# A Trainium2 kernel for channel attention, linear attention and a routed layer: some transposed tiles moved inside SBUF by 16 transfers on two queues, and image 0's loads cut smaller

## The chip, the core and the metric

The kernel runs on one core of one Trainium2 chip. The metric is the device time of one launch in microseconds, the median of several runs. The profile is of one more execution, whose own time stands beside its span.

Short names are those of the profile: PE is the matrix engine (TensorE) and PEld its weight loads, DVE the vector engine, ACT the scalar engine, POOL the GpSimd engine, SP the engine that issues most DMAs. ACT can issue DMAs too. SBUF is the on-chip memory of 128 partitions, PSUM the matmul's accumulator.

## The reference

The input x is four images of 32 channels with 128 by 128 pixels. Layer 0 folds each 2 by 2 patch into channels, normalises an energy matrix, takes a softmax and adds the weighted sum:

```python
xs = x.reshape(B, C, h, R, w, R).transpose(0, 1, 3, 5, 2, 4).reshape(B, C * R * R, h, w)
...
q = xs.reshape(B, C * R * R, hw)
energy = jnp.einsum('bci,bcj->bij', q, q)
d = jnp.sqrt(jnp.diagonal(energy, axis1=1, axis2=2))
energy = energy / (d[:, :, None] * d[:, None, :])
attn = jax.nn.softmax(energy, axis=-1)
out = jnp.einsum('bcj,bij->bci', q, attn).reshape(B, C * R * R, h, w)
out = gamma * out + xs
```

So the energy of an image is 4096 by 4096 and symmetric. Layer 1 takes the result as 4096 tokens of 128 numbers an image, and has a normalised linear attention without softmax, then a second normalisation and a layer of eight experts of which each token takes the two best:

```python
t = t + _L1_attn_ref(_ln_t(t), L1_attn_Wk, L1_attn_Wq, L1_attn_Wv)
t = t + _L1_ffn_ref(_ln_t(t), L1_ffn_router_w, L1_ffn_router_b, L1_ffn_expert_w, L1_ffn_expert_b)
```

## The kernel before

**Layer 0, `attend` (L417).** The 4096 positions of an image are cut into eight columns of 512. For row i (0 to 7) the loop takes the pairs (i, jc) with jc from 0 to i. A pair has four steps j. A step makes one product of 128 by 512 (`pe`, L556), its exponential on ACT (`pr`, L559, with the row sums), and two steps later a matmul of `pr` with the values into `po` (L440). Since the energy is symmetric, the other half of the matrix is the transpose of what is there: for jc < i each `pr` is also transposed in blocks of 32 by 32 by DVE into a tile `F` (L566, the profile shows L369 of a helper), and when the pair is complete the blocks must change places across partitions, which makes the tile `G`. `transposed_share` (L371) then takes four more steps: a matmul with `G` (`pg`, L375) and an ACT instruction that sums `G` (`junk`, L380); the last one adds `pg` to the sum of column jc (L385). The blocks on the diagonal (jc = i) go a smaller way of the same kind (`move_diagonal`, `bring_diagonal`).

**How F becomes G.** `move` (L470) comes two steps after the last `pr` of the pair. It writes `F` to DRAM in one transfer of 1 MiB (`blocks`, L483). Three steps later `bring` (L488) reads it back in four transfers of 256 KiB (L491), each for one quarter of the partitions, in the order that `G` needs. All five are issued by SP. The last image's row 7 has another way for jc of 3 or more (L471 to L481): 16 transfers of 64 KiB from `F` to `G` inside SBUF, all by SP.

**What sets the order.** The order of PE, DVE, ACT and SP is written out by hand: each engine runs its instructions in the order in which the Python loop emits them. `tick` counts steps; `after(n, f)` puts f into the n-th step from now. `clock` counts work in units of a quarter of a matmul: a step of a full pair adds 8, and a step of a transposed share 4 more. A share waits in the list `late` until its due clock, `LAG` = 57 units after `bring`; at most one step of a share goes beside each step of a pair, and the list is first in, first out. `F`, `G` and the DRAM tile `blocks` are rings of 3, 3 and 4 buffers.

**Other work beside it.** The generators in `timed` (L1318 to L1330) are spread over an image: each is given a begin and an end in per cent of the image's clock and a count of turns. Among them are `prep` (loads and norms of the next image, DMAs at L279), `input_rows` (L593; loads the residual T, four parts of 8 rows of tokens, each in four transfers of 128 KiB), and, in image 0 alone, `setup_weights` (46 to 58%) and `setup_sorting` (L136), which fills two DRAM tiles `xs` with rows of x in eight transfers of 624 KiB, DRAM to DRAM, issued by ACT (L154). From 84% on, layer 1 of the image begins (`layer1`) and runs on beside layer 0 of the next one, a turn each 10 units of clock: norms, attention, router, then a sort by expert with indirect DMAs by POOL (L988, L1113), loads of sorted tiles by SP (L1012), products (L1048), stores (L1034), loads of partial sums by ACT (L1089) and the stores of the output (L1095).

The lines that the change touches: L152 to L155 (`xs`), L482 to L486 (`move`), L595 to L596 (`input_rows`), L1325 and L1330 (`timed`).

Of the kernel before, what the change touches and what calls it, by code (L numbers as in the profile page):

```python
# [12 lines left out]
F32 = mybir.dt.float32  # L13
# [9 lines left out]
def kernel(  # L23
# [43 lines left out]
    nc = tc.nc  # L67
    P = 128
    B, C, H, W = x.shape
# [4 lines left out]
    NJ = CH // P  # L74
    HW2 = W // 2
    KT = 32
    S = 32
# [11 lines left out]
    gpool = ctx.enter_context(tc.tile_pool(name="gpool", bufs=3))  # L89
# [29 lines left out]
    NT = 2 * HR + E - 1  # L119
# [6 lines left out]
    xs = [dram.tile([NT * P, D], F32, tag=f"xs{h}", name=f"xs_{h}", bufs=1) for h in range(2)]  # L126
    xs_made, xs_read = ([], []), ([], [])
# [8 lines left out]
    def setup_sorting():  # L136
        def iota(dst, pattern, part=0):
            nc.gpsimd.iota(
                dst, pattern=pattern, base=0, channel_multiplier=part, allow_small_or_imprecise_dtypes=True
            )  # L140

        iota(rank_below, [[1, P]], part=-1)
        nc.vector.tensor_scalar(rank_below, rank_below, 0.0, None, ALU.is_gt)
        iota(upto, [[1, E], [-1, E]])
        nc.vector.tensor_scalar(upto, upto, 0.0, None, ALU.is_ge)
        iota(tiles_of[:, 0, :], [[P, HR]])
        iota(tile_no[:, :, 0], [[1, NT]])
        yield
        yield

        rows = x.rearrange("b c h w -> (b c h) w")
        step = NT * P // 4  # L152
        for g in range(8):
            inst = nc.scalar.dma_start(xs[g // 4][ts(g % 4, step), :], rows[ts(g, step), :])  # L154
            xs_made[g // 4].append(inst.ins)  # L155
            yield
            yield

# [19 lines left out]
    def idle(n):  # L178
        for _ in range(2 * n):
            yield  # L180
# [90 lines left out]
    def tokens(ap, b):  # L271
        return ap[b].rearrange("c (s k r) w -> s r c k w", s=2, r=2)

    def load_tokens(dst, b, k0, nk, queues=(nc.sync, nc.sync)):
        src = tokens(x, b)
        for s in range(2):
            for r1 in range(2):
                p0 = s * 64 + r1 * 32
                queues[r1].dma_start(dst[p0 : p0 + 32], src[s, r1, :, k0 : k0 + nk, :])  # L279
# [72 lines left out]
    clock = [0]  # L352
    tick = [0]
    queued = []
    late = []
    LAG = 57
# [4 lines left out]
    def after(ticks, f):  # L361
        queued.append((tick[0] + ticks, f))
# [8 lines left out]
    def transposed_share(b, st, i, jc, G):  # L371

        pg = ps_g.tile([P, CH], F32, tag="pg", name=f"pg_{b}_{i}_{jc}")
        for ib in range(NJ):
            nc.tensor.matmul(  # L375
                pg.rearrange("p (a f) -> p a f", a=4), st["qT"][i][:, ib, :], G[:, :, ib],
                start=(ib == 0), stop=(ib == NJ - 1),
            )
            junk = work.tile([P, 4, P], BF16, tag="junk", name=f"junk_{b}_{i}_{jc}_{ib}", bufs=1)
            nc.scalar.activation(  # L380
                junk, G[:, :, ib], AF.Copy, accum_out=st["sums"][:, NJ * i + ib, jc : jc + 1]
            )
            if ib == NJ - 1:
                o = st["o"][jc].rearrange("p (j a c) -> p a j c", a=4, c=S)
                nc.vector.tensor_tensor(o, o, pg.rearrange("p (a j c) -> p a j c", a=4, c=S), ALU.add)  # L385
                st["got"][jc] += 1
            yield "done" if ib == NJ - 1 else None
# [29 lines left out]
    def attend(b, st):  # L417
# [11 lines left out]
        for i in range(NCH):  # L429
# [40 lines left out]
            def move(F, i, jc):  # L470
                last = b == B - 1 and i == NCH - 1 and jc >= NCH - 5  # L471
                if last:
                    G = gpool.tile([P, 4, NJ, P], F32, tag="G", name=f"G_{b}_{i}_{jc}")
                    for a in range(4):
                        for q in range(4):
                            nc.sync.dma_start(
                                G[ts(q, S), a].rearrange("p ib f -> p (ib f)"),
                                F[ts(a, S), q].rearrange("p ib j c -> p (ib j c)"),
                            )
                    late.append((clock[0] + 58, transposed_share(b, st, i, jc, G)))  # L480
                    return  # L481
                blocks = dram.tile([4, S, 4, CH], F32, tag="blocks", name=f"blocks_{b}_{i}_{jc}", bufs=4)  # L482
                nc.sync.dma_start(  # L483
                    blocks.rearrange("a p q f -> (a p) q f"), F.rearrange("p q ib j c -> p q (ib j c)")
                )
                after(3, partial(bring, blocks, i, jc))  # L486

            def bring(blocks, i, jc):  # L488
                G = gpool.tile([P, 4, NJ, P], F32, tag="G", name=f"G_{b}_{i}_{jc}")
                for q in range(4):  # L490
                    nc.sync.dma_start(  # L491
                        G[ts(q, S)].rearrange("p a ib f -> p a (ib f)"), blocks[:, :, q].rearrange("a p f -> p a f")
                    )
                late.append((clock[0] + LAG, transposed_share(b, st, i, jc, G)))
# [33 lines left out]
            for jc in order:  # L528
# [15 lines left out]
                if jc < i and not both:  # L544
                    F = fpool.tile([P, 4, NJ, NJ, S], F32, tag="F", name=f"F_{b}_{i}_{jc}")
                    Fb = F.rearrange("p q ib j c -> p ib q j c")
                elif jc == i and not ending:
                    F = fpool.tile([P, 4, 6, S], F32, tag="F", name=f"F_{b}_{i}_{i}")
# [33 lines left out]
    def finish():  # L582

        while queued or late:
            yield
            tick[0] += 1
            turn_tick()
            clock[0] += 3 * NJ
            step_share()
            yield  # L590


    def input_rows(b, st):  # L593
        st["T"] = T = big1.tile([P, KT, D], F32, tag="T", name=f"T_{b}")
        for kc in range(4):  # L595
            load_tokens(T[:, ts(kc, 8), :], b, 8 * kc, 8)  # L596
            yield
            yield
            yield from idle(1)
# [703 lines left out]
    states = [{} for _ in range(B)]  # L1303
# [14 lines left out]
    timed = [(first, 0, 1, 4)]  # L1318
    for b in range(B):

        if b == 0:
            for kc, begin, end in ((1, 0, 5), (2, 6, 20), (3, 25, 45)):
                timed.append((prep(0, kc, states[0]), begin, end, 12))
            timed.append((setup_weights(), 46, 58, 9))
            timed.append((setup_sorting(), 58, 98, 9))  # L1325
        if b + 1 < B:
            nxt = states[b + 1]
            timed.append((prep(b + 1, 0, nxt), 65, 82, 13))
            timed.append((prep(b + 1, 1, nxt), 83, 99, 13))
        timed.append((input_rows(b, states[b]), *((55, 75) if b in (0, B - 1) else (82, 99)), 9))  # L1330
        done = [0] * len(timed)
        start = clock[0]
        closing = None
        for half, _ in enumerate(chain(attend(b, states[b]), finish() if b == B - 1 else ())):
            if half % 2 == 0:
                t = 100 * (clock[0] - start) / UNITS
                moved = []
                if closing is None and t > 84:
                    closing = layer1(b, states[b])
                    steady.append([closing.first_parts() if b == B - 1 else closing.all_parts(), clock[0]])  # L1340
                for n, (steps, begin, end, count) in enumerate(timed):
                    if t >= begin and done[n] * (end - begin) < (t - begin) * count:
                        moved.append(steps)
                        done[n] += 1
                for stream in steady:
                    if clock[0] >= stream[1]:
                        stream[1] = clock[0] + PACE
                        moved.append(stream[0])
            for steps in moved:
                next(steps, None)  # L1350
        for steps, *_ in timed:
            for _ in steps:
                pass
        timed = []
        if b + 1 < B:
            timed.append((prep(b + 1, 2, nxt), 2, 20, 13))
            timed.append((prep(b + 1, 3, nxt), 30, 50, 13))
# [43 lines left out]
```

## Time and profile before

| What | Value |
|---|---|
| Median of 3 runs | 1744.91 us (1744.48 to 1747.42) |
| The profiled execution's own time | 1753.19 us |
| Its span, first to last instruction | 1751.4 us |
| Mean granted TensorE clock | 0.983 |
| Ends of row 7 (`o`, L445) in images 0 to 3 | 378.2, 791.6, 1209.0, 1638.8 us |
| DMA moved | 355.24 MB; HBM read 183.64 MB, written 173.15 MB |
| DMAs by SP's queue (q1) | 314.91 MB, 64.0% of 16 engines' span |
| DMAs by POOL's queue (q0) | 25.19 MB, 5.1% |
| DMAs by ACT's queue (q10) | 13.77 MB, 2.7% |

The page cuts the span in 40 slices and gives a digit for each: the busy share in tenths, and 9 is 90% or more. The list of waits has for each line the engine and its waiting instruction, then what ended the wait, and after the colon the total in us, how often, and the longest. A line of the timeline has the start, the duration in us, engine, line, operation, the tiles (output before the arrow), how many instructions it merges, and in brackets the idle time before and what ended it. SPq and ACTq are DMA issues; their durations are those of the issue, not of the transfer. A wait for several semaphores is put down to the one that came last.

The rows of image 0 end at 21.7, 34.2, 59.6, 97.5, 145.7, 213.5, 294.5 and 378.2 us, those of image 1 from row 4 on at 537.4, 602.4, 690.2 and 791.6, of image 2 at 953.0, 1016.8, 1105.2 and 1209.0, of image 3 at 1369.8, 1434.0, 1527.8 and 1638.8. So the three rows named in the change, 5 to 7, take some 230 to 270 us of each image.

### The profile page before, as it was taken

How to read it: one execution, taken by the hardware profiler on the slowest of the kernel's cores; microseconds unless marked ns; L12 is line 12 of the kernel's file. 1: busy time of each engine (PE TensorE's matmuls, PEld its weight loads, DVE VectorE, ACT ScalarE, POOL GpSimd, SP SyncE). 2: the span in 40 equal slices, each digit the busy share in tenths (PEclk: the TensorE clock that was granted, in tenths of full speed). 3: DMA queues.
4: the chain of work that ended last, by engine and by line, in shares of the span. 5: the costliest groups of instructions: out<-in, count | busy, mean ns of one | idle time of the engine just before them, and what ended most of it. 6: DMA issues, size and time to landing. Idle time of an engine off the chain costs nothing. (4 is left out here: it accounts for less than half of the span.)

```text
span 1751.4 us, 21197 instructions
## 1 busy us (share of the span) xinstructions
PE 1667.8 (95%) x5458; PEld 882.2 (50%) x5458; DVE 939.7 (54%) x2443; ACT 927.0 (53%) x2893; POOL 512.0 (29%) x553
## 2 busy tenths in 40 slices
PE   8999998999999999899999999979999999899887
PEld 5444444455554455445554455535555455444633
DVE  4433333467485335566477334546748533455687
ACT  3555444466565555446565455536556455445376
POOL 1000000011026505540015622552102660463166
PEclk9999999999999999999999999989999999999989
DMA  4675877776568799997567799998656889995001
GB/s 136 195 207 166 217 200 222 237 212 190 165 195 239 232 276 252 264 243 197 164 189 223 227 273 264 251 244 224 192 166 196 251 223 271 265 267 133 1 13 37
DMA packets 240168, 355.24 MB, mean 203 GB/s; under 512 B 26928, under 2 KB 154928, under 8 KB 226096
## 3 DMA queue, kind: packets, MB, share of 16 engines
q1 hardware_dynamic: 219792, 314.91, 64.0%
q0 software_dynamic: 12288, 25.19, 5.1%
q10 hardware_dynamic: 7968, 13.77, 2.7%
q8 instruction: 46, 0.75, 0.2%
q14 instruction: 74, 0.61, 0.1%
HBM read 183.64 MB, written 173.15 MB: 204 GB/s over the span
## 5 line engine op out<-in xcount | busy, mean ns | idle before, releaser
L559 ACT ACTIVATE pr<-pe 128x512 f32<-128x512 f32 (+1 forms) x576 | 322.3, 560 | 546.3 <-PE pe L556 427.9
L440 PE MATMUL po<-pr,qT 128*128 128x512 f32 (+3 forms) x1152 | 553.2, 562 | 3.9 <-ACT o L445 3.5
L375 PE MATMUL pg<-G,qT 128*128 128x512 f32 x880 | 456.8, 601 | 37.5 <-DMA G<-blocks 25.6
L556 PE MATMUL pe<-qn,qn 128*128 128x512 f32 x896 | 464.7, 601 | 1.9 <-ACT pr L559 1.6
L369 DVE STREAM_TRANSPOSE F<-pr 128x512 f32<-128x512 f32 x440 | 305.9, 702 | 169.6 <-ACT pr L559 152.2
L440 PEld LDWEIGHTS po<-pr,qT 128*128 128x128 f32 x1152 | 217.1, 192 | 252.6 <-issue 224.8
L380 ACT ACTIVATE junk<-G 128x512 bf16<-128x512 f32 x440 | 273.1, 621 | 33.9 <-DMA G<-blocks 27.3
L375 PEld LDWEIGHTS pg<-G,qT 128*128 128x128 f32 x880 | 167.3, 192 | 239.6 <-issue 205.8
L1113 POOL DMA_INDIRECT yb<-ys,place x192 | 185.1, 964 | 275.6 <-DMA xn<-xs 103.2
L988 POOL DMA_INDIRECT xs<-xn,place x192 | 185.6, 967 | 125.5 <-issue 51.6
L556 PEld LDWEIGHTS pe<-qn,qn 128*128 128x128 f32 x896 | 156.0, 193 | 113.9 <-issue 103.5
L385 DVE TENSOR_TENSOR o<-o,pg 128x512 f32<-128x512 f32 x110 | 75.4, 685 | 201.4 <-PE pg L375 170.1
L164 POOL TENSOR_TENSOR rn<-ss,neg_half 128x8 f32<-128x8 f32 (+1 forms) x17 | 27.8, 1634 | 401.6 <-DVE ss L325 401.6
L559 ACT ACTIVATION_READ_ACCUMULATOR pr<-pe 128x1 f32 x576 | 112.1, 195 | 0.0
L1022 ACT ACTIVATE xn<-pys 128x256 f32<-128x256 f32 (+1 forms) x120 | 44.9, 376 | 116.1 <-PE pys L1055 69.3
L1048 PEld LDWEIGHTS pys<-ew_sb,xn 128*128 128x128 f32 x468 | 67.9, 191 | 57.2 <-issue 45.3
L164 POOL TENSOR_TENSOR rsf<-dm_f,neg_half 128x8 f32<-128x8 f32 (+1 forms) x15 | 26.2, 1746 | 235.1 <-DVE sv_f L635 235.1
L556 PE MATMUL pe<-qn 128*128 128x512 f32 (+3 forms) x256 | 90.2, 435 | 0.7 <-ACT qn L344 0.7
L380 ACT ACTIVATION_READ_ACCUMULATOR junk<-G 128x1 f32 x440 | 84.4, 192 | 0.0
L1048 PE MATMUL pys<-ew_sb,xn 128*128 x468 | 71.8, 276 | 11.4 <-ACT xn L1022 5.4
L1031 DVE COPY result<-pys 128x256 f32<-128x256 f32 (+1 forms) x60 | 24.6, 410 | 101.6 <-ACT xn L1022 46.2
L164 POOL TENSOR_TENSOR rsa<-dm_a,neg_half 128x8 f32<-128x8 f32 x16 | 26.4, 1647 | 167.4 <-DVE sv_a L635 167.1
(189 smaller groups left out, 1618.5 us busy)
## 6 DMA issues: line engine op xcount, KB each, us to landing
blocks<-F SPq DMA_DIRECT2D x108, 1024.0 KB
G<-blocks SPq DMA_DIRECT2D x432, 256.0 KB
xn<-xs SPq DMA_DIRECT2D x114, 128.0 KB
below<-F SPq DMA_DIRECT2D x31, 384.0 KB
G<-below SPq DMA_DIRECT2D x124, 96.0 KB
T<-in_x_dram SPq DMA_DIRECT2D x64, 128.0 KB
out_dram<-acc SPq DMA_DIRECT2D x128, 64.0 KB
xx<-in_x_dram SPq DMA_DIRECT2D x62, 128.0 KB
```

The lines of the kernel that those rows point to most:

```text
L164: pinned(nc.gpsimd.tensor_tensor(dst, src, neg_half.to_broadcast(list(src.shape)), ALU.pow))
L369: f()
L375: nc.tensor.matmul(pg.rearrange("p (a f) -> p a f", a=4), st["qT"][i][:, ib, :], G[:, :, ib], start=(ib == 0), stop=(ib == NJ - 1),)
L380: nc.scalar.activation(junk, G[:, :, ib], AF.Copy, accum_out=st["sums"][:, NJ * i + ib, jc : jc + 1])
L385: nc.vector.tensor_tensor(o, o, pg.rearrange("p (a j c) -> p a j c", a=4, c=S), ALU.add)
L440: nc.tensor.matmul(row["po"][:, lo:hi], qT[blk // NJ][:, blk % NJ, :], w, start=start, stop=(row["left"] == 0))
L556: nc.tensor.matmul(pe[:, c0:], qn[jc][:, ts(j, P)], qn[i][:, c0:], start=True, stop=True)
L559: nc.scalar.activation(pr[:, c0:], pe[:, c0:], AF.Exp, accum_out=sums[:, t, i : i + 1]).ins
L988: inst = nc.gpsimd.indirect_dma_start(xs[h], offset(place[:, i, k : k + 1]), xn[:, k, :], None)
L1022: nc.scalar.activation(bufs[4 + g % 2][:, :n], p[:, : n * P].rearrange("p (j t) -> p j t", t=P), AF.Copy)
L1048: nc.tensor.matmul(p[:, 2 * P + j * D : 2 * P + j * D + D], bufs[4 + g % 2][:, j, :], weights[:, bass.ds(begins[2 * (g % 2) + j], D)], sta ...
L1113: inst = nc.gpsimd.indirect_dma_start(yb[k // 4][:, i, k % 4, :], None, ys, offset(place[:, i, k : k + 1]))
```

## The change

In rows 5 to 7, a pair with jc of 1, 4 or 7 takes the way inside SBUF (7 never comes, since jc must be below i). It begins one step after `move`, and its 16 transfers go in two halves of eight, a step apart; in each half, numbers 1, 4 and 6 are issued by ACT and the other five by SP. The share is due 8 clock units later than with `LAG`, counted from its earlier start.

In image 0 `xs` is filled in 16 transfers of 312 KiB rather than 8 of 624, and T is loaded in eight parts of 4 rows rather than four of 8, spread over 52 to 94% of the image's clock rather than 55 to 75.

```diff
@@ -149,10 +149,10 @@
-        step = NT * P // 4
-        for g in range(8):
-            inst = nc.scalar.dma_start(xs[g // 4][ts(g % 4, step), :], rows[ts(g, step), :])
-            xs_made[g // 4].append(inst.ins)
+        step = NT * P // 8
+        for g in range(16):
+            inst = nc.scalar.dma_start(xs[g // 8][ts(g % 8, step), :], rows[ts(g, step), :])
+            xs_made[g // 8].append(inst.ins)
@@ -479,11 +479,29 @@
+                if i >= 5 and jc % 3 == 1:
+
+                    after(1, partial(begin_direct, F, i, jc))
+                    return
                 blocks = dram.tile([4, S, 4, CH], F32, tag="blocks", name=f"blocks_{b}_{i}_{jc}", bufs=4)
...
+            def begin_direct(F, i, jc):
+                G = gpool.tile([P, 4, NJ, P], F32, tag="G", name=f"G_{b}_{i}_{jc}")
+                direct_half(F, G, 0)
+                after(1, partial(direct_half, F, G, 2))
+                late.append((clock[0] + LAG + 8, transposed_share(b, st, i, jc, G)))
+
+            def direct_half(F, G, a0):
+                for n in range(8):
+                    a, q = a0 + n // 4, n % 4
+                    (nc.scalar if n in (1, 4, 6) else nc.sync).dma_start(
+                        G[ts(q, S), a].rearrange("p ib f -> p (ib f)"),
+                        F[ts(a, S), q].rearrange("p ib j c -> p (ib j c)"),
+                    )
@@ -592,8 +610,9 @@
         st["T"] = T = big1.tile([P, KT, D], F32, tag="T", name=f"T_{b}")
-        for kc in range(4):
-            load_tokens(T[:, ts(kc, 8), :], b, 8 * kc, 8)
+        nk = 4 if b == 0 else 8
+        for k in range(0, KT, nk):
+            load_tokens(T[:, k : k + nk, :], b, k, nk)
@@ -1322,12 +1341,13 @@
-            timed.append((setup_sorting(), 58, 98, 9))
+            timed.append((setup_sorting(), 58, 98, 17))
...
-        timed.append((input_rows(b, states[b]), *((55, 75) if b in (0, B - 1) else (82, 99)), 9))
+        begin, end, count = (52, 94, 17) if b == 0 else (55, 75, 9) if b == B - 1 else (82, 99, 9)
+        timed.append((input_rows(b, states[b]), begin, end, count))
```

## The prediction

> **What bounds the kernel now.** One core, so the view of cores says only span 1751.4 us, mean clock 0.983. Then the page, parts 1 and 2.
>
> ```profile
> PE 1667.8 (95%) x5458; PEld 882.2 (50%) x5458; DVE 939.7 (54%) x2443; ACT 927.0 (53%) x2893; POOL 512.0 (29%) x553
> ...
> PEclk9999999999999999999999999989999999999989
> DMA  4675877776568799997567799998656889995001
> ```
>
> PE is busy 95%, so only its remaining idle time is for sale, and that lies where DMA reads 8 or 9: late in each image. Next the list of waits, for all engines, then for SP's own queue.
>
> ```profile
> ACT junk L380 <- DMA G<-blocks: 27.3, 14, 6.4
> PE pg L375 <- DMA G<-blocks: 25.6, 11, 6.3
> ```
>
> ```profile
> SPq L491 <- DMA blocks<-F: 270.8, 58, 9.4
> SPq L279 <- DMA acc<-t: 20.9, 4, 7.3
> SPq L483 <- DMA xs<-in_x_dram: 20.9, 2, 15.8
> ```
>
> PE waits for transposed tiles G that have not landed; ACT's wait at L380 is the same event. SP stands 270.8 us at L491 until the DRAM write of a pair has landed, with everything behind it queued. The last two lines are odd: SP waits for transfers ACT issued, whose data it does not need. The records of the DMA instructions explain it: eight completion semaphores (100 to 107) are taken in turn by SP and ACT together, and a new DMA waits until its predecessor on that number has landed. The third step is the timeline of PE, then of SP, round the longest wait.
>
> ```profile
> 1165.39 1.02 PE L440 MATMUL po<-pr,qT 128*128 128x512 f32 x2
> 1172.70 2.04 PE L375 MATMUL pg<-G,qT 128*128 128x512 f32 x2 [6.29 <-DMA G<-blocks]
> 1174.54 1.91 PE L556 MATMUL pe<-qn,qn 128*128 128x512 f32 x2
> ```
>
> ```profile
> 1140.18 3.95 SPq L1095 DMA_DIRECT2D out_dram<-acc  x4
> 1146.76 1.74 SPq L491 DMA_DIRECT2D G<-blocks  x4
> 1148.53 2.81 SPq L279 DMA_DIRECT2D T<-in_x_dram  x4
> 1156.27 0.34 SPq L483 DMA_DIRECT2D blocks<-F  x1
> 1156.73 3.31 SPq L1095 DMA_DIRECT2D out_dram<-acc  x4
> 1162.32 2.09 SPq L491 DMA_DIRECT2D G<-blocks  x4
> ```
>
> A wait costs twice: 6.29 us idle, then matmuls at half speed (1.91 for 1.02). Counting steps of the emission loop against ACT's exponentials (584 of each), the write at 1156.27 belongs to step 414, whose exponential ran at 1136.6: SP is 20 us late. In rows 1 to 4 it runs 1 to 7 us ahead. All waits of PE above 1 us at L375, by place: image 0, row 5, 2.02; row 6, 1.41 and 6.03; image 1, row 7, 2.65, 2.32, 2.42, 1.55, and 1.50 just after; image 2, row 7, 3.85, 1.44, 6.29, and 1.46 after; image 3, row 7, 1.05 and 3.19.
>
> **What the Trainium skill says.** "DMA: Bandwidth & Descriptors", section "Issuing engines are not separate DMA queues": all queues run on the same 16 engines, and a second issuer saves only sequencer time. Here both queues also share the semaphores. Its "Rules for kernel authors" count transfers under 64 KB as mostly overhead; the direct ones are just 64 KB, and SP takes longer to issue them than its 256 KB loads:
>
> ```profile
> 1574.76 1.76 SPq L491 DMA_DIRECT2D G<-blocks  x4
> 1578.94 11.91 SPq L476 DMA_DIRECT2D G<-F  x16
> 1590.95 1.98 SPq L1095 DMA_DIRECT2D out_dram<-acc  x4
> 1593.09 10.15 SPq L476 DMA_DIRECT2D G<-F  x16
> ```
>
> That is 10.15 / 16 = 0.63 us each undisturbed, against 0.44. "TensorE: Matmul & The Clock Gate", section "What's actually happening": an idle array falls to half rate, and about 3.4 us of work brings it back; the trace's clock records show 0.5 for 3.41 us after six of the waits and for 10.24 us at 1168.5.
>
> **Part 1: 23 pairs go direct.** Rows 5, 6, 7 with jc 1 and 4 are six pairs an image; the last image's (7,4) was direct already (line 471), so 23. Each loses a 1 MiB write and a 1 MiB read of DRAM and gains 1 MiB inside SBUF. By the packet records: write 128 packets of 8192 B at 309 ns / 16 engines = 2.5 us; loads 512 of 2048 B at 131 to 145 ns = 4.2 to 4.6; direct 512 of 2048 B at about 122 (1577 to 1612 us, where most packets of that size are direct) = 3.9. So about 3 us of all 16 engines saved per pair, 69 in all; only where DMA is full is that time.
>
> SP per pair: 5 issues (0.36 + 4 x 0.43 = 2.1 us) become 10 x 0.63 = 6.3, 4 more. The wait at L491 goes for these pairs (270.8 / 108 = 2.5 us in the mean, up to 9.4). About even; behind SP stand the loads of the next pair, of T and xx, and the stores. G is allocated two steps earlier (third step after the last j, not fifth), its share due 65 clock units later, not 57: by my count of steps the second half starts 6 steps before its share where the load had 5, and one landing is on the way instead of two. G's ring of three is free one to three steps before, so no new wait there; F's ring likewise.
>
> ACT gets 6 issues per pair, 138 in all. The nearest rows, with minimum, median and maximum in ns:
>
> ```profile
> L1089 ACTq DMA_DIRECT2D acc<-t x24: 326/327/394, 662.6 to 1594.4; - x24
> L154 ACTq DMA_DIRECT2D xs<-in_x_dram x8: 496/501/587, 240.2 to 358.5; - x8
> ```
>
> In ACT's records such an issue starts while the exponential before it still runs (595 ns), and the next activation follows at once. I take 0.33 to 0.63 us each, three per half: 1 to 1.9 us, of which 0.6 lie under the exponential. A step with a transposed share costs ACT 0.60 + 0.19 + 0.62 + 0.19 = 1.6 us of the 2.58 us that three matmuls of 2 x 0.43 us take, and an exponential may be about 3.5 us late before PE waits for its PSUM bank (two banks) or its values (two steps later). So the issues alone are hidden; without that cover they would be up to 23 x 2 x 1.3 = 60 us.
>
> Not hidden is what the ACT issues wait for. Each needs the eighth transfer before it to have landed: for the later ones of the first half these are the four loads of the pair before (L491). Behind the waiting issue on ACT stand the exponential and the copies of layer 1; PE waits for both. If SP is L us late with those loads, landing takes about 6 us, and two steps (6 to 7 us) pass in between: ACT stands about L - 1, PE about L - 5. Lateness in the old trace, last load against its step, for the pairs before the changed ones: image 0: -4.5, 2.9 (row 5), -3.4, 13.3 (row 6), 4.4, 7.4 (row 7); image 1: -4.1, 3.9, 1.9, 2.0, 11.3, 11.5; image 2: -5.2, 2.5, 1.9, 1.9, 12.0, 14.4; image 3: -5.4, 2.4, 5.6, 2.2, 4.1. Bounds: 0 if SP is no longer late, and if it stays so, 8 + 2 (image 0), 6 + 6 (image 1), 7 + 9 (image 2), 1: 39 us, less what this hands back, since PE would have waited for those loads some steps later anyway. I take 8: SP should be less late.
>
> **Part 2: image 0's loads.** T comes in 32 transfers of 64 KB over 52 to 94% of the image, not 16 of 128 KB over 55 to 75%; xs in 16 of 312 KB, not 8 of 624. SP pays 16 x 0.45 = 7 us, spread over 150 us; ACT 8 x 0.5 = 4, under activations. The bytes are the same. The gain is in holding: an xs transfer issued at 255.72 let an xx load go only at 264.28, with the next loads of G behind it at 264.71, and PE stood 6.03 us until 272.26. Half the size holds a semaphore half as long, but there are twice as many on which SP waits for ACT's turn; from 0 to all of that wait is the bound.
>
> **The sum**, on the profiled execution (span 1751.40, with what lies around it 1753.19; it is 8.3 us above the median 1744.91, so waits may be smaller without the profiler).
> - Image 0: row 5's wait, 2.02 + 3.41 x 0.5 = 3.7 us, goes: the share at 184.9 is a changed pair's, and its data would leave before the weights that ACT loads at 172.9. Row 6, 1.41 + 6.03 and half of the slow 5.4 us = 10.1: I take two thirds, 6.8. Together 10.5.
> - Images 1 and 2: idle 10.4 and 13.0 us; slow stretches 3 x 3.41 and 3.41 + 6.1 us at half rate, 5.1 and 4.7. Together 33. By row 7's waits three changed pairs have gone by, 9 us of DMA time per image. SP gives 4 us per pair back in issues, and its lateness is a matter of both: a third, 11.
> - Image 3: nothing; its last wait stands behind the direct pairs that were there.
> - ACT: +8.
> Net -13.5: 1753.2 to 1739.7 under the profiler. For the median, with smaller waits, I take -12: **1733 us**. Late next are the products of the sorted tiles (L1048, idle 11.4 us on the page) and the shares after (7,1).
>
> **Rivals.**
> A, the forecast: some of G's waits go, 1724 to 1741. Chance 0.52.
> B, nearly all go: 3 us per pair also empty the queue in row 6, SP enters row 7 on time, ACT never waits. 13.9 + 20 - 2 = 32 off: 1713. For it: images 0 and 3 have rows where lateness up to 8 us costs nothing, so it is a matter of a few us. Against: SP's longer issues. Chance 0.14.
> C, no change: the 3 us saved and the 4 us of issue cancel, the loads of T only move to row 7: 1744. For it: DMA is full with T, the stores and the indirect transfers too. Chance 0.13.
> D, slower: ACT becomes tied to SP. In row 7 of images 1 and 2, the third step after jc 1 and jc 4, ACT stands until loads that SP issues 11 to 14 us late have landed. It decides from about 5 us of lateness. 39 us, less half of the 33 that are then already waited for = 22; image 0's loads give 10 back: 1757. For it: SP stood 15.8 us at one L483 for a transfer of ACT's, so the tie is real in one direction. Against: the ACT issues of the old kernel in row 7 (L1089) stand at most some 1.5 us. Chance 0.21.
>
> **Numbers.** A gain or loss under 0.2% (3.5 us) can't be told from none here. Faster: A, B and a little of C, 0.68; same 0.10; slower: D and a little of C, 0.22. The range, 1716 to 1757, leaves out half of B and half of D. A's own range is given above.
>
> **What would show it.** Right: G<-F from SP and ACT in rows 5 to 7, about 24 MB less each of HBM read and write, PE's waits at L375 in image 0 gone and in row 7 of images 1 and 2 smaller, SP's wait at L491 down by a fifth. Wrong: waits of PE at L556 or L440 for exponentials that come after an ACT issue; idle stretches of ACT ahead of the new line; SP as late in row 7 as before, or waiting for G<-F; a clock of 0.5 in places where it was full.

## The result and the profile after

| | Before | After |
|---|---|---|
| Median of 5 runs, us | 1744.91 (1741.17 to 1747.42) | 1757.02 (1756.56 to 1759.73) |
| Ratio | | 1.0072, interval 1.0053 to 1.0091 |
| Profiled execution, own time / span, us | 1753.19 / 1751.4 | 1759.73 / 1757.9 |

The change makes the kernel 0.7% slower; 12 us faster was forecast. The two profiled executions differ by 6.5 us, about half of what the medians do: that of the kernel before lay 8.3 us above its median, that of the kernel after 2.7. So the trace shows the place of the loss better than its full size. In two later series the same kernel gave 1.0065 (1.0045 to 1.0085) and 1.0079 (1.0056 to 1.0103).

First the page of the kernel after: busy times, the granted clock and the DMA share in 40 slices, and what moved through HBM.

```profile
PE 1667.5 (95%) x5458; PEld 883.5 (50%) x5458; DVE 941.1 (54%) x2443; ACT 927.8 (53%) x2893; POOL 513.2 (29%) x553
...
PEclk9999999999999999999999999999999999999999
DMA  5675777665676878886577778897656687885001
...
HBM read 159.52 MB, written 149.03 MB: 176 GB/s over the span
```

The engines do the same work. HBM carries 24.1 MB less each way, as 23 pairs of 1 MiB should give, and the row of DMA digits, which had 8 and 9 late in each image, is thinner. The engines that move the data have more room than before, and yet the end is later. So what was gained is not what was missing.

Next the list of PE's waits after: who waits, for what, then the sum in us, how often, the longest.

```profile
PE pys L1067 <- DVE result L1050: 17.5, 3, 6.4
PE pg L375 <- DMA G<-blocks: 16.0, 8, 3.7
PE pys L1074 <- DMA xn<-xs: 6.7, 4, 2.3
...
PE pg L375 <- DMA G<-F: 5.3, 4, 2.1
```

The waits for `G` through DRAM fell from 25.6 us to 16.0. Another line has come to the top: three waits of PE at L1067, the products of layer 1's sorted tiles, for DVE's copy of a `result`, 17.5 us. Before, at the old L1048, it was

```profile
PE pys L1048 <- DVE result L1031: 4.3, 2, 3.9
```

And the list of the SP queue's own waits after:

```profile
SPq L509 <- DMA blocks<-F: 241.0, 65, 9.5
...
SPq L509 <- DMA G<-F: 85.2, 19, 12.3
...
SPq L1031 <- DMA G<-F: 23.4, 8, 8.4
```

SP now also waits for transfers from `F` to `G`, at lines that do not use them: 135.4 us over all lines, and all of it for transfers that ACT issued. Whether that is the cost is tried below.

**Where the time went.** I cut both traces at the last output of each row (`o`, L445). In us:

| Row, us | Image 0 | Image 1 | Image 2 | Image 3 |
|---|---|---|---|---|
| 5, before / after | 67.8 / 65.1 | 65.0 / 62.0 | 63.8 / 62.3 | 64.2 / 62.0 |
| 6, before / after | 81.1 / 72.9 | 87.8 / 97.1 | 88.5 / 96.1 | 93.8 / 99.7 |
| 7, before / after | 83.6 / 88.6 | 101.3 / 101.2 | 103.7 / 101.6 | 111.0 / 112.4 |

Row 6 of images 1, 2 and 3 loses 9.3 + 7.6 + 5.9 = 22.8 us. Everything else gains 16: image 0 5.7, row 5 of the others 6.7, their rows 0 to 4 3.2, row 7 0.8. Row 6 of image 1, by the view of windows: stretch, its length, then busy time and number of instructions of PE, PEld, DVE, ACT and POOL, the clock, the DMA share and GB/s. Before:

```profile
602.40:690.20 87.80, 87.80 (x351) 51.24 (x350) 40.68 (x84) 45.55 (x141) 25.17 (x25) 1.00 0.95 262
```

After:

```profile
593.70:690.80 97.10, 90.74 (x348) 52.44 (x347) 40.66 (x86) 45.50 (x142) 25.21 (x26) 0.96 0.77 216
```

This pair of lines is the case in small. Before, PE never stopped in this row (87.80 busy of 87.80, clock 1.00) though DMA was at 0.95. After, DMA is down to 0.77, PE stands still for 97.10 - 90.74 = 6.4 us, and the clock falls to 0.96. The stretch of PE and DVE where that happens, after:

```profile
641.75 0.42 DVE L1050 COPY result<-pys 128x256 f32<-128x256 f32 x1 [0.17 <-ACT xn L1041]
...
647.72 1.02 PE L375 MATMUL pg<-G,qT 128*128 128x512 f32 x2
...
654.66 0.29 DVE L1050 COPY result<-pys 128x128 f32<-128x128 f32 x1 [9.64 <-DMA ys<-result]
...
655.10 1.19 PE L1067 MATMUL pys<-ew_sb,xn 128*128 x4 [6.36 <-DVE result L1050]
...
656.51 1.91 PE L574 MATMUL pe<-qn,qn 128*128 128x512 f32 x2
```

Read it from below. PE's product waits 6.36 us for DVE, which had to empty the PSUM bank; afterwards matmuls run at half speed (1.91 for 1.02 us; the clock's records show 0.5 for 6.83 us from 653.6). DVE's copy waits 9.64 us for a store `ys<-result`, because `result` has two buffers. And that store belongs to the copy at 641.75. The issues of SP show when it left:

```profile
626.48 3.04 SPq L501 DMA_DIRECT2D G<-F  x5
...
631.25 3.90 SPq L501 DMA_DIRECT2D G<-F  x5
635.20 2.09 SPq L279 DMA_DIRECT2D xx<-in_x_dram  x4
...
638.86 0.45 SPq L487 DMA_DIRECT2D blocks<-F  x1
...
645.02 1.86 SPq L509 DMA_DIRECT2D G<-blocks  x4
646.98 0.38 SPq L1053 DMA_DIRECT2D ys<-result  x1
...
648.87 0.83 SPq L487 DMA_DIRECT2D blocks<-F  x1
```

The copy ended at 642.2 and its store was issued at 646.98, behind a queue that has hardly a gap from 623 to 650; it landed at 654.57. Before, in the same place:

```profile
648.69 1.86 SPq L491 DMA_DIRECT2D G<-blocks  x4
650.87 0.38 SPq L1034 DMA_DIRECT2D ys<-result  x1
```

There the copy had run at 650.42, so its store left as it ended. The next copy had to wait then too, 4.43 us until 656.67, but PE had other work for that long and never noticed. From the end of its copy to its landing the store took 12.4 us after and 5.7 before: 4.8 of the difference are that SP comes later, 1.9 that the transfer itself takes longer. For the write of the pair (6,2), which stands in SP's queue right behind the moved pair (6,1), the lateness (issue against the exponential of its step) goes from 1.7 to 10.1 us in image 1, 2.2 to 9.2 in image 2 and 5.8 to 10.5 in image 3. SP's issues in row 6 of image 1 add up to 60.7 us, 47.0 before. The other two long waits for a `result`, 5.2 and 6.0 us, stand in row 6 of images 2 and 3.

### The profile page after: what moved, and what is told of

It reads as the page before. It is cut to its first block, busy times and chain, and to the rows that moved or that the text cites. A ratio compares the mean times of both kernels' runs of the same rounds, so it can differ in the third digit from the quotient of the medians.

```text
span 1757.9 us, 21523 instructions
## 1 busy us (share of the span) xinstructions
PE 1667.5 (95%) x5458; PEld 883.5 (50%) x5458; DVE 941.1 (54%) x2443; ACT 927.8 (53%) x2893; POOL 513.2 (29%) x553
## 5 line engine op out<-in xcount | busy, mean ns | idle before, releaser
L375 PE MATMUL pg<-G,qT 128*128 128x512 f32 x880 | 453.9, 598 | 26.2 <-DMA G<-blocks 16.0
L375 PEld LDWEIGHTS pg<-G,qT 128*128 128x128 f32 x880 | 167.8, 193 | 227.2 <-issue 184.5
L1067 PEld LDWEIGHTS pys<-ew_sb,xn 128*128 128x128 f32 x468 | 69.8, 195 | 63.8 <-issue 59.8
L164 POOL TENSOR_TENSOR rsf<-dm_f,neg_half 128x8 f32<-128x8 f32 (+1 forms) x15 | 26.2, 1746 | 235.0 <-DVE sv_f L654 235.0
L1067 PE MATMUL pys<-ew_sb,xn 128*128 x468 | 73.0, 280 | 17.6 <-DVE result L1050 17.5
```

The source lines that it names most:

```text
L164: pinned(nc.gpsimd.tensor_tensor(dst, src, neg_half.to_broadcast(list(src.shape)), ALU.pow))
L375: nc.tensor.matmul(pg.rearrange("p (a f) -> p a f", a=4), st["qT"][i][:, ib, :], G[:, :, ib], start=(ib == 0), stop=(ib == NJ - 1),)
L1067: nc.tensor.matmul(p[:, 2 * P + j * D : 2 * P + j * D + D], bufs[4 + g % 2][:, j, :], weights[:, bass.ds(begins[2 * (g % 2) + j], D)], sta ...
```

## The experiments

Each series ran beside the kernel before, whose time differs from series to series, by its medians: 1758.87 us (loads alone, moved pairs alone, row 6 as before, 16 loads), 1744.66 (half on ACT, all on SP, two results, all on POOL), 1746.34 (the two mixtures with POOL), 1763.65 and 1744.91 us (repeats). So ratios are compared, in brackets their 95% interval. Edits are against the kernel after.

**Which part, and where.** Three kernels take the change apart.

Image 0's loads alone:

```diff
-                if i >= 5 and jc % 3 == 1:
+                if False:
```

> Image 0's smaller loads alone, no pair goes inside SBUF. All theories put the loss into the moved pairs, so this should be a little faster than before: in the profile after, image 0 ended 5.7 us earlier with both parts. About 1739 us, row 7 of image 0 ending near 373 us instead of 378, images 1 to 3 as before (row 6: 88, 88, 94 us). 1750 or more would mean that the loads themselves cost.

Measured 0.9975 (0.9958 to 0.9993).

The moved pairs alone:

```diff
-        step = NT * P // 8
-        for g in range(16):
+        step = NT * P // 4
+        for g in range(8):
...
-        nk = 4 if b == 0 else 8
+        nk = 8
...
-            timed.append((setup_sorting(), 58, 98, 17))
+            timed.append((setup_sorting(), 58, 98, 9))
...
-        begin, end, count = (52, 94, 17) if b == 0 else (55, 75, 9) if b == B - 1 else (82, 99, 9)
+        begin, end, count = (55, 75, 9) if b in (0, B - 1) else (82, 99, 9)
```

> The moved pairs alone, image 0's loads as before. Theory SP (SP's long issues make layer 1's stores late in row 6): row 6 of images 1 to 3 as in the changed kernel, 97, 96 and 100 us, and 1760 us or a little over, as image 0's waits of row 6 are back in part. Theory ACT (ACT's issues wait for late loads of SP, in row 7): the same total, but the loss in row 7.

Measured 1.0124 (1.0101 to 1.0146), row 6 of images 1 to 3 at 97.6, 95.2 and 98.6 us. Against the loads alone that is 20 us more in row 6, and rows 5 and 7 of these images are longer too, by 8 and 11 us.

Both, but row 6 as before:

```diff
-                if i >= 5 and jc % 3 == 1:
+                if i in (5, 7) and jc % 3 == 1:
```

> The changed kernel with rows 5 and 7 moved and row 6 left as before. Theory SP: row 6 of images 1 to 3 back at 88, 88, 94 us, so some 20 us less than the changed kernel: about 1736 us, faster than before. Theory ACT: row 7 holds the loss and keeps it: 1752 to 1757 us. Theory route (transfers inside SBUF are slow for everybody): a third of the loss goes, 1753 us.

Measured 0.9972 (0.996 to 0.9983); row 6 at 88.6, 88.9 and 94.8 us. The loss seems to lie in the pairs of row 6 alone. But in this series the kernel before took 14 us longer than beside the change, and the changed one had not run there. So it was run once more:

> The kernel with row 6 as before, once more. When it first ran, the kernel before had a median of 1758.87 us beside it, 14 us more than in the other comparisons, and the changed kernel did not run there, so the two ratios, 0.9972 and 1.0072 or 1.0065, came from different surroundings. If the whole loss is made by the moved pairs of row 6, the ratio is again 0.995 to 0.999, with row 6 of images 1 to 3 at 88 to 95 us. If the first ratio was low only because the kernel before was slow there, the ratio is 1.003 to 1.007 (the time near 1753 us against 1745), and part of the loss lies outside row 6: in the moved pairs of rows 5 and 7.

Measured 0.9958 (0.9944 to 0.9972), but again beside a long time of the kernel before (1763.65 us), so the doubt stayed. Then the three ran in one series:

> The changed kernel beside the two that take it apart, for the first time on one chip in one series. If the moved pairs of row 6 make the whole loss, it is 0.8 to 1.2% slower than the kernel with row 6 as before that runs after it. If a part of that difference was one of chips, it is 0.2 to 0.6%.

> The kernel with row 6 as before. If row 6 makes the whole loss, its ratio is 0.994 to 0.999, whatever the time of the kernel before; if a part of it lies in the pairs of rows 5 and 7, it is over the loads alone by 0.3% or more.

> Image 0's loads alone: 0.995 to 0.999 if they gain what they gained at first. At 1.002 or more their gain would be one of the first chip only, and the loss of the changed kernel would be theirs too.

| On one chip, before 1744.91 us | Median, us | Ratio | Row 6, images 1 to 3, us |
|---|---|---|---|
| The change | 1759.00 | 1.0079 (1.0056 to 1.0103) | 96.2, 95.2, 97.8 |
| Row 6 as before | 1731.19 | 0.9931 (0.9907 to 0.9955) | 88.3, 88.3, 92.8 |
| Loads alone | 1740.31 | 0.9972 (0.996 to 0.9984) | 88.2, 88.0, 92.6 |

That settles the place. The pairs of row 6 cost 1.0079 / 0.9931 = 1.5%, more than was expected of them; 19.8 us of it stand in the three rows 6 of the two traces. The loads gain 0.3%, and the moved pairs of rows 5 and 7 bring another 0.4%, which the first series had not shown (0.9972 with them, 0.9975 without). Row 5 is at 62.0 us in images 1 to 3 in all three kernels, so its gain is not one of the moved pairs.

**What of a moved pair costs.** A moved pair differs from an old one in four things: bytes inside SBUF instead of through DRAM, six issues on ACT, ten issues on SP instead of five, and sixteen turns at the semaphores that SP and ACT share instead of five. The next kernel keeps the old way and all of its bytes, leaves ACT alone, and only reads each changed pair back in 16 loads of 64 KiB, all by SP:

```diff
-                if i >= 5 and jc % 3 == 1:
+                if False:
...
+                many = i >= 5 and jc % 3 == 1
                 for q in range(4):
-                    nc.sync.dma_start(
-                        G[ts(q, S)].rearrange("p a ib f -> p a (ib f)"), blocks[:, :, q].rearrange("a p f -> p a f")
-                    )
+                    for a in range(4) if many else ():
+                        nc.sync.dma_start(G[ts(q, S), a].rearrange("p ib f -> p (ib f)"), blocks[a, :, q])
+                    if not many:
+                        nc.sync.dma_start(
+                            G[ts(q, S)].rearrange("p a ib f -> p a (ib f)"), blocks[:, :, q].rearrange("a p f -> p a f")
+                        )
```

> The smaller loads of image 0, no pair inside SBUF, but in the pairs that the change moves the four loads from DRAM become sixteen of 64 KB, all issued by SP. ACT issues nothing more, the bytes are the same. Theory SP: 17 issues of 0.4 to 0.6 us instead of 5, row 6 of images 1 to 3 longer by 5 to 9 us each, 1755 to 1765 us. Theories ACT and route: as with the loads alone, about 1740 us.

Measured 1.0216 (1.0188 to 1.0244). Its list of PE's waits begins:

```profile
PE pg L375 <- DMA G<-blocks: 36.9, 15, 5.0
PE pys L1071 <- DVE result L1054: 10.4, 3, 3.9
```

With 17 issues on SP for a pair the loss is larger than that of the change, without a byte inside SBUF and without ACT. But most of it is elsewhere: row 6 is at 96.5, 93.9 and 92.9 us, 12 us more in sum than with the loads alone, while row 7 of these images has 17 us more and image 0 15. And the sixteen loads also take their turns at the shared semaphores, which this kernel does not separate from the issues.

Then the change with all 16 transfers on SP, which takes ACT out of it and leaves the number of transfers, and so of turns of the semaphores, as it is:

```diff
-                    (nc.scalar if n in (1, 4, 6) else nc.sync).dma_start(
+                    nc.sync.dma_start(
```

> The changed kernel with all 16 inner transfers issued by SP, none by ACT. Theory SP's issue time: 6 x 0.6 = 3.6 us more per pair on SP, so row 6 loses half as much again, ratio to before 1.011 to 1.016. Theory semaphores: as the changed kernel, 1.007. Theory ACT: the loss goes with ACT's issues, below 1.003.

Measured 1.0196 (1.0174 to 1.0218), above what any theory said, and far from the 1.007 and the 1.003 or less that the theories of shared semaphores and of ACT asked for. PE's waits:

```profile
PE pg L375 <- DMA G<-blocks: 18.2, 9, 4.2
PE pys L1067 <- DVE result L1050: 16.0, 3, 6.1
PE pg L375 <- DMA G<-F: 12.1, 6, 4.7
PE pys L1074 <- DMA xn<-xs: 10.9, 4, 3.8
```

All that comes through SP is later: tiles of both kinds, results, sorted tiles. In this run the list of SP's waits has none for a `G<-F` transfer, where the kernel after had 135 us of them, and it is slower by another 1.2%. So these waits across the queues, conspicuous as they are, are not needed for such a loss. Row 6, however, did not lose half as much again, as the theory of SP's issue time asked: it is at 95.7, 95.3 and 95.9 us, 6 us less in sum than after. The further loss is in image 0 (10 us) and in row 7 of the others (8).

The opposite step gives half of the transfers to ACT:

```diff
-                    (nc.scalar if n in (1, 4, 6) else nc.sync).dma_start(
+                    (nc.scalar if n % 2 else nc.sync).dma_start(
```

> The changed kernel with every other inner transfer issued by ACT: 8 of 16 instead of 6. Theory SP's issue time: SP gives up 2 of its 10 issues, 1.2 us a pair of the 4 it gained, so a fifth to a third of the loss of row 6 goes, ratio to before about 1.004 to 1.005. Theory semaphores (a transfer takes one of the eight in turn, whoever issues it): unchanged, 1.007. Theory ACT: worse, 1.009 or more, with PE waiting for exponentials.

Measured 1.0059 (1.004 to 1.0079), which the total can't tell from the kernel after. Row 6 can: 92.9, 94.4 and 94.7 us, 11 us less in sum than after, and 7 less than in the shortest of its three profiles. Over all of these, in the order of SP's issues for a pair, with how late SP is at the write of (6,2), as above, and the length of row 6, both summed over images 1 to 3 (the kernel before: 9.7 us late, 270.1 us long):

| Kernel | SP | ACT | Ratio | SP late, us | Row 6, us |
|---|---|---|---|---|---|
| loads alone, old way | 5 | 0 | 0.9975, 0.9972 | 11.8, 9.2 | 271.1, 268.8 |
| half on ACT | 8 | 8 | 1.0059 | 23.9 | 282.0 |
| the change | 10 | 6 | 1.0072, 1.0065, 1.0079 | 29.8, 29.5, 29.6 | 292.9, 290.1, 289.2 |
| all on SP | 16 | 0 | 1.0196 | 28.2 | 286.9 |
| old way, 16 loads | 17 | 0 | 1.0216 | 24.7 | 283.3 |

The whole time rises with the number of SP's issues. Row 6 does not: it goes with how late SP is. And ten issues on SP beside six on ACT make SP as late there as sixteen on SP alone. An estimate from the traces says why. In the three rows 6 the change adds 2 x 3.8 us of issues a row, 23 in sum, and SP waits 23.6 us for transfers of ACT; with all on SP the issues add 2 x (16 x 0.588 - 2.1) a row, 44 in sum, and there is no such wait. So in the change about half of what SP takes on in row 6 would be its own issues and half its waits for ACT's transfers. The same estimate gives 16 and 16 us with half on ACT, and 30 and none with 16 loads; in both SP is less late than in the other two.

**The wait at the end of it.** If the ring of two `result` buffers is the place, two results in one buffer of double size should free it. (They were two buffers of one result; now two of two.)

```diff
-                            result = work.tile([P, 2, D], F32, tag="grp", name=f"result_{b}_{h}_{g}", bufs=2)
+                            if g % 4 == 2:
+                                two[:] = [work.tile([P, 2, 2, D], F32, tag="grp", name=f"result_{b}_{h}_{g}", bufs=2)]
+                            result = two[0][:, g % 2]
...
-            begins = []
+            begins, two = [], []
```

> The changed kernel, but two results of the sorted products share one buffer of the ring of two, so the ring holds four results instead of two, and a result no longer waits until the store of the last but one has landed. If SP's lateness reaches PE through this ring (stores of results late, then the copy, then the product at L1067), the wait of 5 to 6 us and the half-rate stretch after it go from row 6 of images 1 to 3: 7 to 9 us each, ratio to before 0.993 to 0.997. If PE stands at the next late transfer instead: 1.004 or more.

Measured 1.0053 (1.0036 to 1.007): a miss. The wait did go, and another one came for it, as PE's list says:

```profile
PE pys L1076 <- DMA xn<-xs: 20.3, 8, 4.4
PE pg L375 <- DMA G<-blocks: 12.4, 6, 4.1
```

PE stands at the same products, now for the sorted tiles that SP loads. Row 6 is at 94.2, 94.6 and 98.1 us, 6 us less in sum than after and 2 less than in its shortest profile, and SP is as late as there (29.8 us in sum). The buffer was where the lateness showed, not where it came from.

**Another queue.** If SP's time is what lacks, a queue with room should take the transfers at no cost. All 16 by POOL:

```diff
-                    (nc.scalar if n in (1, 4, 6) else nc.sync).dma_start(
+                    nc.gpsimd.dma_start(
```

> The changed kernel with all 16 inner transfers issued by POOL, which has completion semaphores of its own and is little used in row 6. Theories SP's issue time and semaphores: both loads are off SP, and its wait for the DRAM write too, so row 6 falls under that of before: ratio 0.990 to 0.998. Theory route (the engines are slow with transfers inside SBUF): row 6 stays at 95 to 100 us, 1.005 or more.

Measured 1.006 (1.0042 to 1.0077), but with the loss in another place. The window of row 6 in image 1:

```profile
592.00:681.10 89.10, 87.97 (x348) 51.03 (x347) 39.53 (x82) 45.62 (x142) 41.91 (x60) 1.00 0.86 231
```

1.1 us idle instead of 6.4, clock 1.00. Row 6 is at 89.1, 88.3 and 86.4 us: the loss there is gone, and SP comes to the write of (6,2) at -1.1, 0.4 and 0.0 us. The bytes go inside SBUF as in the change, so that way itself is not what cost row 6. Row 7 is at 107.6, 111.6 and 118.4, from 101.2, 101.6 and 112.4. Its cause, in POOL's timeline of image 1, row 7:

```profile
759.49 4.00 POOL L501 DMA_DIRECT2D G<-F  x8
763.79 1.00 POOL L1132 DMA_INDIRECT yb<-ys,place  x1 [0.30 <-issue]
...
768.60 1.68 POOL L164 TENSOR_TENSOR rsa<-dm_a,neg_half 128x8 f32<-128x8 f32 x1
770.36 0.20 POOL L656 TENSOR_TENSOR nba<-sv_a,rsa 128x8 f32<-128x8 f32 x1
```

The second eight issues of (7,4) hold POOL for 4.00 us (the first eight, with waits, had taken 6.6), the gathers of layer 1 come behind them, and two small operations of the next norm behind those; PE's `pgram` then waits 10.93 us for ACT's `xn`, which waits for `nba`. So POOL was kept for rows 5 and 6 and for image 0, and row 7 of the others left as before the change:

```diff
-                if i >= 5 and jc % 3 == 1:
+                if (i in (5, 6) or i == 7 and b == 0) and jc % 3 == 1:
...
-                    (nc.scalar if n in (1, 4, 6) else nc.sync).dma_start(
+                    nc.gpsimd.dma_start(
```

> As the kernel with POOL's issues, but row 7 of images 1 to 3 goes by DRAM as before: there POOL's issues stood ahead of the small operations of layer 1's first norm, for which PE waited 10.9, 7.1 and 4.2 us at pgram. Theory SP's queue (SP must not have more issues, and where they go must have room): row 6 of images 1 to 3 stays at 86 to 89 us, row 7 back at 101 to 104 and 111, pgram's waits gone: ratio to before 0.983 to 0.990, faster than both kernels. If the waits of row 7 come whatever is issued: 1.000 or more.

Measured 0.9958 (0.9942 to 0.9975), 1740.86 us: a gain, less than half of the one expected. The waits at `pgram` went (2.6 us are left, as before the change). Row 7 fell only to 104.1, 102.5 and 112.5 us, and PE waits for `G` through DRAM 21.6 us again in the whole kernel. The last step moves (7,1) too, and leaves only (7,4) of images 1 and 2 in the old way:

```diff
-                if i >= 5 and jc % 3 == 1:
+                if (i in (5, 6) or i == 7 and (b == 0 or jc == 1)) and jc % 3 == 1:
...
-                    (nc.scalar if n in (1, 4, 6) else nc.sync).dma_start(
+                    nc.gpsimd.dma_start(
```

> As the last, with the pair (7,1) of images 1 to 3 on POOL too, and only (7,4) by DRAM. The gathers of layer 1 are on POOL from the end of row 6 on; eight microseconds of issues among them come 50 us before the norm's operations. If only issues right ahead of the norm hurt: row 7 some 2 us shorter than in the last kernel, 0.982 to 0.989. If POOL is full all through row 7: 0.990 to 0.997.

Measured 0.9917 (0.9898 to 0.9936), 1730.4 us: faster than both kernels, and about as fast as the one with row 6 left as before (0.9931). The ratio lies where it was expected for a POOL that is full all through row 7, but row 7 is at 94.8, 97.2 and 113.1 us, in images 1 and 2 more than the 2 us shorter that was named for the other case. PE's waits:

```profile
PE pbd L740 <- DVE rdx L718: 7.2, 3, 2.8
PE pgram L694 <- ACT xn L662: 6.0, 3, 2.6
...
PE pg L375 <- DMA G<-blocks: 3.9, 3, 2.4
```

The wait for `G` through DRAM, 25.6 us before the change, is 3.9, and the wait for `result` is 1.5 us. The changed kernel itself, run once more in the series of these two:

> The changed kernel once more, beside these two on one chip: 1.005 to 1.009 of before.

Measured 1.0065 (1.0045 to 1.0085), row 6 at 96.7, 95.2 and 98.0 us. The loss and its place come back.

## Why the prediction was wrong

**Right.** The bytes came out as worked out. Image 0 gains: row 6 is 8.2 us shorter where 6.8 were taken, row 5 2.7 of 3.7; row 7 gives 5.0 back, which leaves 5.7 of the 10.5. This gain is the loads': with them alone image 0 gains 9.2 and 6.7. PE's idle time at L375 fell from 37.5 to 26.2 us. The issues on ACT are hidden as issues: the three of a half start 0.0, 0.6 and 1.2 us after their step in the median, and with them on SP the kernel gets worse. And with row 6 left out the change gains 13.7 us in the last series, as much as was forecast for all of it, though not in the places named.

**The step that failed: "About even."** SP's issues for a moved pair were worked out as 4 us more, and set against 2.5 us of a wait at L491 that goes. The first was well sized. The durations of the new issues, minimum, median and maximum in ns, are

```profile
L501 SPq DMA_DIRECT2D G<-F x230: 507/588/1692, 172.7 to 1572.9; - x115
L501 ACTq DMA_DIRECT2D G<-F x138: 514/602/1355, 168.4 to 1563.9; - x138
```

so 10 x 0.588 - 2.1 = 3.8 us more. The second was a mean over all pairs, and it measured less: SP's wait for the DRAM writes fell by 270.8 - 241.0 = 29.8 us, 1.3 for each of 23 pairs, a ninth and not a fifth. And a term was left out: 85 us of waits for `G<-F` came at the same line, 135 over all. That SP waits for transfers of ACT because both take their semaphores in turn had been read from the old trace, and "waiting for G<-F" stands among the signs of being wrong; but the sum priced the tie for ACT alone.

Above all the balance was struck per pair and not per stage. In row 6 SP carries some 70 other issues, most of layer 1, and there it had no slack: it was 1.7 to 5.8 us late before, and is 5 to 8 us later behind the first moved pair. PE had shown no idle time in row 6 of images 1 and 2 (0.0 and 0.5 us). But that means only that nothing was late enough to be seen: DVE's wait of 4.43 us was there, just hidden. The row cost 22.8 us where nothing was allotted.

The sum said -13.5 for the profiled execution and the trace has +6.5, 20 apart: 22.8 are row 6; 8.8 are gains missing in row 7 of images 1 and 2, 4.8 in image 0; row 7 of image 3 adds 1.4. Against them stand the 8 set for ACT, whose small cost is in row 7, and 9.9 by which rows 0 to 5 of images 1 to 3 came out shorter, for which the sum had no term.

**Named but not priced.** "Late next are the products of the sorted tiles" was the right place in the code, given as what comes after the gain, with no term in the sum. It came instead of the gain: PE's idle time ahead of `pys` grew from 11.4 to 24.4 us.

**"A third, 11"** for row 7 of images 1 and 2 measured 0.1 + 2.1. As they were issued here, the transfers that save bytes hardly helped there; in the kernel with (7,1) and rows 5 and 6 on POOL the same two rows are 6.5 us shorter each than before.

The Trainium skill, "DMA: Bandwidth & Descriptors", section "Issuing engines are not separate DMA queues", was cited for a second issuer saving only sequencer time; the page adds that this is usually small beside the transfer. In a stage whose queue is nearly full it is not small: SP's issues take 60.7 of the 97.1 us of row 6 in image 1, and with the sixteen on POOL row 6 of images 1 to 3 is 29 us shorter in sum.

**"ACT: +8"** measured little, though it did occur. In row 7 of image 2, at the third step after (7,1), where Rival D had placed it, ACT stands until an earlier transfer has landed, and PE waits for the exponential behind:

```profile
1137.29 4.11 ACTq L501 DMA_DIRECT2D G<-F  x2
1141.45 0.42 ACT L400 ACTIVATE junk<-G 128x256 bf16<-128x256 f32 x1 [4.11 <-DMA G<-F]
...
1143.02 1.13 PE L574 MATMUL pe<-qn,qn 128*128 128x512 f32 x2 [1.46 <-ACT pr L577]
```

This is the only wait of PE over 0.4 us for an exponential behind such an issue in the trace, and the row as a whole got shorter. (The wait of 3.6 us for `pr_back` in row 7 of image 3 is as long with all on SP, 3.3, so it is not one of ACT's issues.) Rival D therefore had the sign and the tie, and with 1757 by chance the number: it put the loss in row 7, on ACT. The tie cost more in the other direction, SP standing for ACT, and the loss was made in row 6, by SP's lateness. With all on SP, where D's cost is gone, the kernel is slower still.

**Open.** Why the issue of 64 KiB inside SBUF takes SP 0.588 us when that of 64 KiB from DRAM, in the kernel with 16 loads, has a median of 0.419. How SP's lateness in row 6 divides between its issues and its waits for ACT's transfers is estimated above, not shown: no kernel has ten issues on SP and six elsewhere with semaphores of their own. By which waits the pairs of rows 5 and 7 gain their 0.4%, which one series of two shows. And the chain from SP to PE was followed link by link in image 1 alone.

## What to carry to other kernels

A queue's issues are work on an engine like any other: before a transfer is split, count all issues of its queue in that stage times their duration, also where the compute engine shows no idle time, and look for waits of the other engines that are only just hidden. Where two queues take the same semaphores in turn, price the waits in both directions. How late a queue reaches one fixed transfer, read from each trace, told these kernels apart better than the count of issues. Moving transfers to a queue with room can turn a loss into a gain (here 1.0065 into 0.9917, with one pair of a row left out), if the small operations that stand behind them on that engine are looked up first. Removing the last link of a chain that is late, such as a buffer, uncovers the next late link; the cause is where the lateness enters.

## What the hardware showed beyond what was expected

An issue of a 64 KiB transfer inside SBUF takes POOL less time than SP or ACT. POOL's line in the kernel with all of them on POOL:

```profile
L501 POOL DMA_DIRECT2D G<-F x368: 496/498/775, 167.7 to 1566.1; - x184
```

That is 0.498 us in the median, against 0.588 on SP and 0.602 on ACT, which reach 1.692 and 1.355 at most, POOL's 0.775. On SP the issue of a load from DRAM has about the same length for a quarter of the bytes (0.419 us for 64 KiB, 0.430 for 256 KiB in the same kernel), so splitting a load in four cost SP nearly four times as much. And the time of the kernel before differed by 1% between series (medians of 1744.66 to 1763.65 us; the first two, 14 us apart, were on one chip), and the others did not follow in proportion: the kernel with row 6 as before gave 0.9972, 0.9958 and 0.9931. Parts of a change are best compared in one series.
